# The state-space mixer of a decoder layer in chunks of 64 tokens, two chunks in the partition halves

## The chip, the core and the metric

The kernel runs on one core of one Trainium2 chip. The time is the device time of one launch in microseconds, from the first to the last instruction and what the launch lays around them; smaller is better. The core has five engines that run side by side[...]: TensorE (PE, with the weight load shown apart as PEld), VectorE (DVE), ScalarE (ACT), GpSimd (POOL) and SyncE (SP), which here only issues transfers. The on-chip memory has 128 partitions; TensorE writes to PSUM, eight banks of 2 KB a partition. All data are float32.

## What is computed

One decoder layer on x of 4 x 1024 tokens and 256 features, in three stages, each followed by the addition of its input and a layer norm without weights:

1. a mixer with 16 heads of 16 channels and a state of 64, which is the part that changes;
2. cross attention over 77 context tokens, with a mask;
3. a feed-forward of 256 to 1024 to 256 with relu.

The mixer in the reference, cut to what matters:

```
logA = einsum(W_logA, x) + b_logA                 # one number per token and head
XBC  = silu(einsum(W_XBC, x) + b_XBC)             # X: 16, B: 64, C: 64 per token and head
cum  = cumsum(logA over the tokens)
A    = where(causal, exp(cum_i - cum_j), 0)       # per head, 1024 x 1024
G    = einsum('bihn,bjhn->bhij', C, B)
Y    = einsum('bhij,bjhc->bihc', A * G, X)
out  = (gate * Y) @ W_out.T + b_out               # gate is linear in x
```

No 1024 x 1024 matrix has to be built. The tokens are cut into chunks: inside a chunk the product A * G is formed as it stands, and what earlier chunks contribute is carried by a state of 64 x 16 per head, which decays by the exponential of the chunk's last cum and takes in the chunk's own B and X.

## The kernel before

**Tiling.** The 4096 tokens are 16 units of T = 256 tokens, four to a batch. In the mixer a unit has NC = 2 chunks of P = 128 tokens. `stage_a(u)` is the mixer, `stage_b(u)` the attention, `stage_c(u)` the feed-forward of unit u.

**Order.** Nothing is ordered by the loops. Every piece of work is a small function that `part(u, name)` puts on a list with a place: u plus the number that `WHEN[name]` holds, or `EDGE[u][name]` for units 0, 1 and 15. The list is sorted by place and the functions are called in that order, so that each engine gets its instructions in it. Place is counted in units: a name at -0.7 is issued 0.7 of a unit before the unit's number. Several units are in flight at once, and the matmuls of the feed-forward of one stand between the mixer's steps of another. Waits between engines are put in from the tiles' reads and writes. PSUM is one pool of eight banks (`bank`).

**The steps of the mixer**, with their lines in the old kernel:

- `pl` (589), `cum` (600): logA for all heads, tokens along the free axis, and its running sum on VectorE, each chunk from 0. Partition 64 c + 32 k + h holds head h of group k in chunk c.
- `cd`, `dl` (606 to 623): cum goes out to DRAM and comes back broadcast to all partitions: `dl` is 128 (token j) x 8 heads x 128 (token i) for a chunk c and a group k of 8 heads. `ce`, `ec` (611 to 633): the same values by head and channel, for the decay of the state's part.
- `pcum`, `ncum` (636, 643): -cum with tokens on the partitions, as a bias.
- `ex`, `sel` (787, 796): exp(cum_i - cum_j) per head on ScalarE, in place, and zeros above the diagonal on GpSimd.
- `pb`, `th`, `bct` (661 to 690): B and C by a matmul, and silu on ScalarE and VectorE. A `bct` tile holds two heads, 64 rows each.
- `pg` (806), `st` (818): G for a chunk and a group of 8 heads, and the product with A on VectorE. B is loaded as weights, C moves. A matmul has 64 rows, one of two heads, so two run on the array's two row halves; 128 columns move.
- `ptb`, `bk` (825, 833): B turned, tokens on the partitions. `xw` (772): X times the decay to the end of the chunk.
- `pc`, `sn` (857, 870): the chunk's own part of the new state, and the new state as the old one decayed plus that part. `pts`, `new` (883, 893): the state turned and copied, in the form in which `pyo` needs it as weights.
- `pyo`, `py` (842, 904): the old state times C, and X times (A * G). Weights are 128 rows x 32 columns, so four run side by side on the array's column quarters; 128 columns move.
- `ya`, `yg`, `poa`, `r1` (916 to 945): the two parts added, the gate, the output projection, the residual.

The state is stepped once a chunk, twice a unit; `states[chunk % 2]` and `statesT[chunk % 2]` are the old one, the other two the new one. At a batch's first chunk there is no old state (`first`), at its last no new one is made (`last`).

**Shapes of the array.** A matmul is given a tile of the 128 x 128 array by the rows of its weights (128, 64 or 32) and by their columns (128, 64 or 32). Consecutive matmuls on different tiles of one shape can run side by side.

## Time and profile before

| | |
|---|---|
| median of 3 runs | 707.78 us (707.65 to 707.82) |
| the profiled execution | 708.88 us |
| its span, first to last instruction | 707.2 us |
| mean granted TensorE clock | 0.99 |
| instructions | 19482 |
| HBM read, written | 55.50 MB, 6.29 MB |

The costliest groups of TensorE besides the feed-forward (busy us, number of passes): pg 70.0, 1024; pb 43.5, 1024; pe 35.5, 512; ptb 35.2, 224; py on dl 34.8, 1024; pa 34.2, 512; py on the state 18.1, 448; pc 17.9, 448; pts 11.0, 56. The feed-forward's pf and ph take 121.5 and 120.1, with 512 passes each.

How to read it: the page is one execution. Busy times of TensorE contain the time in which a matmul is only on its way through the array, so that neighbours overlap and the sum of the lengths is more than the time; the start times tell how fast matmuls follow each other. A share of busy time is a mean over the span. Idle time of an engine other than the one that sets the end costs nothing.

### The profile page before, as it was taken

How to read it: one execution, taken by the hardware profiler on the slowest of the kernel's cores; microseconds unless marked ns; L12 is line 12 of the kernel's file. 1: busy time of each engine (PE TensorE's matmuls, PEld its weight loads, DVE VectorE, ACT ScalarE, POOL GpSimd, SP SyncE). 2: the span in 40 equal slices, each digit the busy share in tenths (PEclk: the TensorE clock that was granted, in tenths of full speed). 3: DMA queues.
4: the chain of work that ended last, by engine and by line, in shares of the span. 5: the costliest groups of instructions: out<-in, count | busy, mean ns of one | idle time of the engine just before them, and what ended most of it. 6: DMA issues, size and time to landing. Idle time of an engine off the chain costs nothing.

```text
span 707.2 us, 19482 instructions
## 1 busy us (share of the span) xinstructions
PE 676.7 (96%) x7744; PEld 536.2 (76%) x7744; DVE 542.9 (77%) x1336; ACT 414.9 (59%) x1091; POOL 276.9 (39%) x448
## 2 busy tenths in 40 slices
PE   0888999999999999999999999999999999999996
PEld 0556777877878787887878788787878888787785
DVE  1469989687878787887977787887878788786662
ACT  0566877557575674738577565846666474763210
POOL 0533353433344353334444344334425333443241
PEclk9989999999999999999999999999999999999999
DMA  4464573314131232413321231342322122100001
GB/s 110 111 192 145 161 231 130 79 62 127 61 112 62 69 97 69 144 60 110 102 76 68 93 111 61 83 135 78 107 96 84 65 79 76 39 9 9 16 8 38
DMA packets 40438, 63.05 MB, mean 89 GB/s; under 512 B 6095, under 2 KB 29340, under 8 KB 40348
## 3 DMA queue, kind: packets, MB, share of 16 engines
q1 hardware_dynamic: 38880, 61.40, 28.2%
q8 instruction: 61, 1.00, 0.6%
q10 hardware_dynamic: 1468, 0.41, 0.3%
q14 instruction: 29, 0.24, 0.1%
HBM read 55.50 MB, written 6.29 MB: 87 GB/s over the span
## 4 chain that ended last, share of the span: by engine, by line
PE 91%; DVE 5%; DMA 2%; issue 1%; POOL 1%; SPq 0%; POOLq 0%; ACT 0%; DVEq 0%
PE pf L1157 16%; PE ph L1130 16%; PE pg L813 9%; PE pb L668 5%; PE pe L1039 5%; PE pa L1064 4%; PE po_b L1100 4%; PE pq L967 4%; PE po_a L937 4%; PE py L910 4%; PE ptb L831 4%; PE pm L992 3%; PE px L730 2%; PE py L849 2%; PE pgt L697 2%; PE pc L864 2%
## 5 line engine op out<-in xcount | busy, mean ns | idle before, releaser
L791 ACT ACTIVATE dl<-dl,ncum 128x128 f32<-128x128 f32 x512 | 156.0, 393 | 8.2 <-DVE de L763 8.2
L1157 PE MATMUL pf<-w,hT 128*128 128x256 f32 x512 | 121.5, 382 | 0.0
L1130 PE MATMUL ph<-T_c,w 128*128 128x256 f32 x512 | 120.1, 381 | 0.0
L799 POOL TENSOR_SCALAR_AFFINE_SELECT dl<-dl 128x1024 f32<-128x1024 f32 x64 | 70.1, 1095 | 112.7 <-ACT dl L791 103.4
L1130 PEld LDWEIGHTS ph<-T_c,w 128*128 128x128 f32 x512 | 95.1, 190 | 14.6 <-issue 2.5
L1157 PEld LDWEIGHTS pf<-w,hT 128*128 128x128 f32 x512 | 93.7, 190 | 13.1 <-issue 1.8
L1050 ACT ACTIVATE es<-pe,mb 77x512 f32<-77x512 f32 x128 | 77.0, 680 | 45.3 <-PE pe L1039 44.1
L688 DVE SCALAR_TENSOR_TENSOR bct<-th,pb 128x512 f32<-128x512 f32 x128 | 81.7, 679 | 9.0 <-ACT th L680 8.9
L838 ACT COPY bk<-ptb 128x512 f32<-128x512 f32 x56 | 32.8, 586 | 92.8 <-PE ptb L831 92.7
L823 DVE TENSOR_TENSOR dl<-pg,dl 128x512 f32<-128x512 f32 x128 | 80.9, 682 | 6.7 <-PE pg L813 4.9
L680 ACT ACTIVATE th<-pb 128x512 f32<-128x512 f32 x128 | 69.3, 591 | 23.0 <-PE pb L668 19.1
L813 PE MATMUL pg<-bct 64*128 64x128 f32 x1024 | 70.0, 284 | 0.5 <-DVE bct L688 0.4
L813 PEld LDWEIGHTS pg<-bct 64*128 64x128 f32 x1024 | 62.5, 191 | 9.3 <-DVE mv_b L542 2.5
L1003 DVE TENSOR_REDUCE maxes<-pm 128x4 f32<-128x308 f32 x128 | 52.2, 470 | 14.4 <-PE pm L992 14.3
L1146 ACT ACTIVATE hT<-ph,b 128x256 f32<-128x256 f32 x64 | 26.7, 471 | 48.8 <-PE ph L1130 47.7
L547 POOL TENSOR_SCALAR rs_a<-mv_a 128x1 f32<-128x1 f32 x32 | 7.3, 228 | 113.4 <-DVE mv_a L542 113.4
L931 POOL TENSOR_TENSOR yg<-ya,gT 128x256 f32<-128x256 f32 x28 | 21.7, 776 | 67.4 <-DVE ya L924 51.9
L668 PE MATMUL pb<-xt,w_bc 17*64 17x256 f32 x1024 | 43.5, 408 | 1.6 <-DVE dl L823 1.4
L1082 POOL TENSOR_TENSOR on<-at,rec 128x256 f32<-128x256 f32 x32 | 19.8, 618 | 46.3 <-DVE rec L1077 44.5
L668 PEld LDWEIGHTS pb<-xt,w_bc 17*64 17x64 f32 x1024 | 22.6, 137 | 18.6 <-issue 9.9
L831 PE MATMUL ptb<-ident,bct 128*128 128x128 f32 x224 | 35.2, 282 | 1.3 <-DVE dl L823 1.2
L1039 PE MATMUL pe<-qm,kT 32*77 32x256 f32 x512 | 35.5, 389 | 0.0
(124 smaller groups left out, 1214.5 us busy)
## 6 DMA issues: line engine op xcount, KB each, us to landing
dl<-cd SPq DMA_DIRECT2D x64, 512.0 KB
xt<-in_xT_dram SPq DMA_DIRECT2D x64, 64.0 KB
xu<-in_xT_dram SPq DMA_DIRECT2D x16, 256.0 KB
ec<-ce SPq DMA_DIRECT2D x16, 256.0 KB
xk<-in_x_dram SPq DMA_DIRECT2D x16, 256.0 KB
out_dram<-r SPq DMA_DIRECT2D x32, 128.0 KB
w<-in_w_dram SPq DMA_DIRECT2D x2, 1024.0 KB
cd<-cum SPq DMA_DIRECT2D x16, 64.0 KB
```

The source lines that it names most:

```text
L668: nc.tensor.matmul(pbs[r][64 * half : 64 * half + 64, bc, :], lhsT=w_bc[rs, 2 * gk + half, bc, :], rhs=xt[rs, 2 * gk + half, :], start=Tru ...
L680: nc.scalar.activation(th, s[f"pb{gk}"][r], AF.Tanh)
L688: nc.vector.scalar_tensor_tensor(t, s[f"th{gk}{r}"], 1.0, s[f"pb{gk}"][r], ALU.add, ALU.mult)
L791: nc.scalar.activation(dl[:, h, :], dl[:, h, :], AF.Exp, bias=s["ncum"][:, 2 * c + k, h : h + 1],)
L799: nc.gpsimd.affine_select(out=dl, in_=dl, compare_op=ALU.is_ge, fill=0.0, base=0, pattern=[[0, 8], [1, P]], channel_multiplier=-1,)
L813: nc.tensor.matmul(pgs[half][:, r, :], lhsT=t[lo : lo + 64, 0, cs], rhs=t[lo : lo + 64, 1, cs], start=True, stop=True,)
L823: nc.vector.tensor_tensor(d, v[f"pg{k}"][half], d, ALU.mult)
L831: nc.tensor.transpose(v[f"ptb{k}"][:, r, :], s["bct"][4 * k + r][:, 0, cs], ident)
L1039: nc.tensor.matmul(pes[r][:, par, :], lhsT=kT[rs, gp, par, bs], rhs=s["qm"][rs, par, gp, :], start=True, stop=True,)
L1050: nc.scalar.activation(e, s[f"pe{gp}"][r], AF.Exp, bias=mb[:, b : b + 1], scale=CH**-0.5)
L1130: nc.tensor.matmul(ph[:, j, :], lhsT=w1[:, k, f * P : (f + 1) * P], rhs=s["xT"][:, k, :], start=(k == 0), stop=(k == 1),)
L1157: nc.tensor.matmul(pf, lhsT=s["hT"][:, f, c * P : (c + 1) * P], rhs=w2[:, f, :], start=(f == 0), stop=(f == FF // P - 1),)
```

## The change

The mixer's chunk becomes L = 64 tokens. Two chunks are handled together, one in each half of the partitions: c still counts 128 tokens, and a new index q counts its halves.

- `pl` and `cum`: one partition group of 32 for each of the four chunks of a unit, all 16 heads in it, 64 tokens along the free axis. `pl` sums two matmuls per chunk.
- `dl`: one tile per c for all 16 heads, 128 x 2 x 8 x 64: the partitions 64 q to 64 q + 63 get the chunk 2 c + q. Two transfers of 256 KB each. `ec`: two transfers instead of one, same size in sum.
- `pcum`: instead of one transposition, two matmuls with columns of the identity, one into each half of the partitions.
- `ex`: as many instructions, 64 columns each. `sel`: two instructions per (c, k), one for each half of the partitions.
- `pg`: a matmul has 64 rows (one of two heads) and 64 columns of weights (the tokens of one half), and 64 columns move: array quarters. Twice as many. `st`: two instructions per c instead of four, of the same size.
- `pc`: weights of 64 rows x 32 columns: array eighths, 128 columns move, twice as many, into two banks. `sn`, `pts`, `new`: the state is stepped for q = 0 and then q = 1: four steps a unit. `ptb`, `bk` and `xw` are no longer left out in a batch's last chunk, where the step for q = 0 is still made.
- `py`: weights of 64 rows x 32 columns, 64 columns move: eighths, twice as many, into two banks. `pyo`: weights of 128 rows x 32 columns as before, 64 columns move, twice as many. The half q = 1 uses the state that this same c made for q = 0.
- `ya`: two instructions per q, four per c, each of half the size.
- `states`, `statesT`: two halves each. `dl` has 4 buffers of the same size instead of 5 with one tile per c instead of two.
- `WHEN` and `EDGE`: all numbers are new, those of the attention and the feed-forward too. Among them: the context's loads and the first of its values stand ahead of the mixer's first inputs.

The core of the diff:

```diff
+L = 64
@@ chunk_a
-        old, new = states[chunk % 2], states[(chunk + 1) % 2]
-        so, sn = statesT[chunk % 2], statesT[(chunk + 1) % 2]
+        old, new = states[(chunk + 1) % 2], states[chunk % 2]
+        so, sn = statesT[(chunk + 1) % 2], statesT[chunk % 2]
+        before = [(None if first else old[:, 1], None if first else so[:, 1]), (new[:, 0], sn[:, 0])]
+        kept = range(1 if last else 2)
...
+        @part(u, f"pg{c}")
+        def _():
+            pgs = v["pg"] = [bank([P, 2, 4, L], f"pg_{n}_{a}") for a in range(2)]
+            for k in range(2):
+                for r in range(4):
+                    t = s["bct"][4 * k + r]
+                    for a in range(2):
+                        for q in range(2):
+                            ts = slice(c * P + q * L, c * P + q * L + L)
+                            nc.tensor.matmul(
+                                pgs[a][L * q : L * q + L, k, r, :],
+                                lhsT=t[64 * a : 64 * a + 64, 0, ts],
+                                rhs=t[64 * a : 64 * a + 64, 1, ts], start=True, stop=True,
+                            )
...
+        @part(u, f"pc{c}")
+        def _():
+            v["pc"] = [bank([P, 2, P], f"pc_{n}_{q}") for q in kept]
+            for k in range(2):
+                for q in kept:
+                    js = slice(L * q, L * q + L)
+                    for r in range(4):
+                        nc.tensor.matmul(
+                            v["pc"][q][32 * r : 32 * r + 32, k, :],
+                            lhsT=v["xw"][js, 4 * k + r].rearrange("p a c -> p (a c)"),
+                            rhs=v[f"bk{k}"][js, r, :], start=True, stop=True,
+                        )
+        @part(u, f"sn{c}")
+        def _():
+            for q in kept:
+                if before[q][1] is None:
+                    nc.vector.tensor_copy(sn[:, q], v["pc"][q])
+                    continue
+                for k in range(2):
+                    nc.vector.scalar_tensor_tensor(
+                        sn[:, q, k, :], before[q][1][:, k, :], s["ec"][:, k, c, q, L - 1 : L],
+                        v["pc"][q][:, k, :], ALU.mult, ALU.add,
+                    )
...
+        @part(u, f"pyo{c}")
+        def _():
+            py = pys()
+            for q in range(2):
+                if before[q][0] is None:
+                    continue
+                for k in range(2):
+                    for r in range(4):
+                        nc.tensor.matmul(
+                            py[q][32 * r : 32 * r + 32, 0, k, :],
+                            lhsT=before[q][0][:, 4 * k + r].rearrange("n a c -> n (a c)"),
+                            rhs=s["bct"][4 * k + r][:, 1, c * P + q * L : c * P + q * L + L],
+                            start=True, stop=True,
+                        )
+        @part(u, f"py{c}")
+        def _():
+            py = pys()
+            for k in range(2):
+                for half in range(2):
+                    for q in range(2):
+                        js = slice(L * q, L * q + L)
+                        for r in range(4):
+                            nc.tensor.matmul(
+                                py[q][32 * r : 32 * r + 32, 1, k, :],
+                                lhsT=xz[js, half, 4 * k + r, :],
+                                rhs=s[f"dl{c}"][js, k, 2 * r + half, :],
+                                start=(half == 0), stop=(half == 1),
+                            )
```

## The prediction

> **What bounds the kernel now.** I read the page from the top: the engine shares, then the slices, then one stretch in the middle, then the rows of one engine in order of time.

> ```profile
> span 707.2 us, 19482 instructions
> PE 676.7 (96%) x7744; PEld 536.2 (76%) x7744; DVE 542.9 (77%) x1336; ACT 414.9 (59%) x1091; POOL 276.9 (39%) x448
> PE   0888999999999999999999999999999999999996
> PE 91%; DVE 5%; DMA 2%; issue 1%; POOL 1%; SPq 0%; POOLq 0%; ACT 0%; DVEq 0%
> ```

> TensorE is busy from the second slice to the last, and 91% of the chain that ended last is TensorE. The busy times of the stretch 267.02 to 308.13, which is one of the 16 units (the same place in the order comes round again after 41.1 us), in the order PE, PEld, DVE, ACT, POOL, clock, DMA share, GB/s:

> ```profile
> 267.02:308.13 41.11, 41.11 (x505) 33.12 (x497) 32.55 (x83) 26.23 (x69) 16.27 (x25) 1.00 0.28 91
> ```

> TensorE has no idle time in it, at full clock; VectorE, the next, has 8.5 us to spare. So only what TensorE does, or would newly wait for, moves the time. Its rows (start, length):

> ```profile
> 341.75 1.89 PE L1157 MATMUL pf<-w,hT 128*128 128x256 f32 x8
> 343.57 0.81 PE L992 MATMUL pm<-km,q 32*128 32x154 f32 x16
> 344.31 1.99 PE L1157 MATMUL pf<-w,hT 128*128 128x256 f32 x8
> 346.24 0.81 PE L992 MATMUL pm<-km,q 32*128 32x154 f32 x16
> 346.97 1.08 PE L910 MATMUL py<-dl,xz 128*32 128x128 f32 x32
> 347.87 0.62 PE L864 MATMUL pc<-bk,xw 128*32 128x128 f32 x16
> 348.42 2.06 PE L813 MATMUL pg<-bct 64*128 64x128 f32 x32
> 350.40 0.66 PE L1016 MATMUL pmt<-ident,maxes 128*128 128x128 f32 x4
> ```

> Lengths contain the pipeline; what counts is start to start. A float32 matmul is two passes (32 records for 16 matmuls of pg). Passes on different tiles of the array start 7 ns apart and run side by side; then the next round follows. From the starts of single records: a full-array pass over 256 columns takes 216 ns, a round of 154 columns 130, of 128 columns 109, so 0.84 ns a column and 2 more. px and pg take 112[...]. Check: py, 8 rounds of four at 109, is 0.87 us; the next row starts 0.90 later.

> A change of tile shape costs extra. pf, 8 passes x 216 = 1.73, but pm starts 1.82 later; pm, 4 rounds x 130 = 0.52, but pf starts 0.74 later: 0.31 for two changes. pg, 16 x 112 = 1.79, then 1.98: 0.19. Pairs of neighbours give 0.12 to 0.22; I take **0.17 us**. py to pc, one shape, costs nothing.

> The whole: all rounds make 603 us, and 290 changes of shape (counted in the program's order) 49; the other 55 are the first 16 us, a ragged start up to 60 us, and the tail.

> **The change, part by part, on TensorE.** A round of 64 columns should take 2 + 64 x 0.84 = 56 ns, 58 where it also loads 64 columns.

> - pg: 16 rounds of two tiles a chunk become 16 of four, 64 columns long. 512 x (112 - 58) = **-27.6**.
> - py on dl: 8 rounds of four become 8 of eight. 256 x (109 - 56) = **-13.6**. Eight starts at 6.8 ns fill 54 of these 56 ns.
> - py on the state: 112 rounds of 109 become 240 of 56 (half 1 of a batch's first chunk now has one): **+1.2**.
> - pc: 112 rounds of four become 112 of eight and, in four last chunks, 16 of four, still 128 columns: **+1.8**.
> - pts: four transposes a chunk for two, 120 for 56: 64 x 109 = **+7.0**. ptb no longer skips a batch's last chunk: 32 x 109 = **+3.5**.
> - pl and pcum: twice the matmuls, half the columns or fewer: 0.

> Sum of rounds **-27.7**. Then the shapes. py on dl (64 rows x 32 columns) and on the state (128 x 32) no longer share one, and pc and pcum get their own: 373 changes for 290. 83 x 0.17 = **+14.1** (10 to 18 by the two ends). No profile row names this cost; it takes half of the gain.

> **Waits.** TensorE's separate semaphore waits go from 193 to 319. At 16 us, where four stand close together, they are 126 to 165 ns apart. If all 126 new ones were bare: +16. But in the middle of the run about 18 pairs of load and matmul are ahead of such a wait, which covers 0.25 us even at the new pace; I take **+3** (0 to 16).

> New in kind is the chain inside a chunk: pc, sn, pts, new, then the state product of half 1 of the same chunk. By rows: four sn steps at 0.30 (14.4 us for 48), pts 0.44 and 0.27 to drain, two copies at about 0.35: 2.6 us. The state had half a unit before; now, in the order built, pq, po_b, ptb and pm (about 4 us) stand between pc and pts, and po_b, pc of the other chunk and py (about 2) between pts and the product. The 4 us cover sn if VectorE comes to it within 2.8; the 2 us cover drain and copies (1.0) if ScalarE is free within 1. I take 0; uncovered by 1 us in 32 chunks, +32. The old trace has one such wait:

> ```profile
> PE pts L889 <- DVE stateT L878: 0.6, 1, 0.6
> ```

> **Other engines**, all beside TensorE. VectorE: st halves (64 of 682 ns fewer: wall -40), sn +19 (64 more steps at 0.30), ya +13 (four instructions of half size for two), the scan -3: 532, still 8 us free a unit. ScalarE: 512 exponentials of 64 columns for 128, about 40 ns less each, -20; more bk and a larger new, +8. GpSimd: 128 selects on half the partitions for 64, about as long in sum, and 4 more xw. dl is fetched in 64 transfers of half the bytes, ec in two per unit instead of one; DMA is at 28%. None of it decides unless TensorE gets a wait.

> **The start.** The order is new: on SP eight loads for the keys and values now stand ahead of xt and xu, and a later transfer waits for the one eight before it (k_b waited 5.5 us for v_w's load, issued at 8.4, to 17.4). So pl comes later than 16.0; but keys, values, and the projections of later units now stand before the first pg and fill what was ragged. I take **+2** (-5 to +8).

> Sum: -27.7 + 14.1 + 3 + 2 = **-8.6**: 698.6 for a span of 707.2. That run took 708.9, the median is 707.8; from the median, **699**.

> [...] The row first: passes on different tiles start 7 ns apart, in py four at a time. [...] What the row leaves open is a long run: no 64 passes in the old trace stand closer than 27 ns on average, while py now asks for 7. One place bounds the supply: after a wait that ended at 116.735 us TensorE's queue put out 12 pairs in 168 ns, so 14 ns a pair or less.

> **Rivals.**
> - *Supply of instructions* (17%). pg, pc and the state product have 14 ns a pair, py only 7. At 14 ns py gains nothing: +14, **713**; over 11.2 ns the kernel is slower than before. For it: 3344 more pairs in bursts never seen; against: the 12 pairs.
> - *The chain of states is late* (16%). 0.3 us in each of 32 chunks eats the gain; 0.5 us gives **715**. For it: two state steps in a row where there was one; against: the slack above.
> - *Quarters run two at a time* (8%), so that the change doesn't do what it says: pg then takes 32 rounds of 58, +29.7, **728**. Against it: pb already runs eight tiles side by side.
> - *More is hidden* (12%): cheap changes of shape (0.12) and a denser start: **688**.
> - My sum (47%), its own range 690 to 707.

> Within 0.2% (1.4 us, about what a measurement tells from no change) lies 0.04 from the edge of my sum's range. Faster: 0.44 of mine, all of the fourth, and 0.03 of a chain that is late by little, 0.59; slower 0.37. The range reaches to the first three: 685 to 728.

> **What would show it.** Right: pg's block of 64 records is followed 0.95 to 1.15 us later by its neighbour, py's on dl 0.45 to 0.65 later; a unit takes 40.2 us with TensorE still full. Supply: py's starts 10 ns or more apart. Chain: waits of pts on stateT or py on state in every unit. The start: the first slices show PE later than 16 us. The forecast is wrong if the middle unit exceeds 41.1 us, whatever the cause.

## The result, and the profile after

The kernel became slower by a third of a per cent: 709.87 us (708.38 to 713.34, 15 runs) for 707.82 (706.34 to 708.32, 15 runs) of the kernel before on the same chip, ratio 1.0035 with a 95% interval of 1.0021 to 1.0049. The forecast was 699. The runs after are also spread wider, 5.0 us for 2.0. The profiled execution took 708.51 us.

The page of the changed kernel, the lines that answer to those of before:

```profile
span 706.8 us, 26495 instructions
PE 665.4 (94%) x11088; PEld 524.1 (74%) x11088; DVE 515.3 (73%) x1402; ACT 403.4 (57%) x1107; POOL 296.0 (42%) x525
PE   1768979999999999999999999999999999999996
PE 90%; DMA 4%; issue 2%; DVE 1%; POOL 1%; SPq 0%; POOLq 0%; ACT 0%; ACTq 0%
```

The second, third and sixth slices lie lower than before (a slice is 17.7 us). The chain now has 4% of DMA for 2% before, and 2% of "issue" for 1%: time for which the profile names no wait. One unit in the middle, with the columns as before:

```profile
296.04:336.04 40.00, 40.00 (x691) 31.78 (x683) 30.75 (x85) 24.98 (x70) 17.79 (x32) 1.00 0.24 71
```

This unit takes 40.0 us, where the one shown before took 41.1, with TensorE full. It looks as if the middle gave what was forecast (40.2), but the units are not alike: at a batch's end the old kernel leaves some work out, and its units there take 39.5 and 40.7 us. A fair comparison is a whole batch, from the first pq of a unit to the first pq four units later, before and after:

```profile
296.94:459.37 162.43, 162.43 (x1931) 130.79 (x1930) 131.11 (x326) 103.32 (x274) 66.54 (x106) 1.00 0.28 87
296.04:456.75 160.71, 160.71 (x2774) 127.82 (x2767) 124.47 (x341) 100.54 (x276) 71.25 (x125) 1.00 0.22 64
```

That is 1.7 us a batch, or 0.43 a unit, half of the 0.85 that the sum of rounds and shapes promised. TensorE's rows in the unit:

```profile
305.92 0.31 PE L643 MATMUL pcum<-ident,cum 128*64 128x32 f32 x4
306.16 1.16 PE L834 MATMUL pg<-bct 64*64 64x64 f32 x64
307.25 1.22 PE L674 MATMUL pb<-xt,w_bc 17*64 17x256 f32 x32
...
310.40 0.60 PE L1030 MATMUL pmt<-ident,maxes 128*128 128x128 f32 x4
310.93 0.86 PE L923 MATMUL py<-dl,xz 64*32 64x64 f32 x64
311.72 0.65 PE L908 MATMUL py<-bct,state 128*32 128x64 f32 x32
312.31 1.99 PE L1144 MATMUL ph<-T_c,w 128*128 128x256 f32 x8
```

pg to its neighbour is 1.09 us, inside the forecast's 0.95 to 1.15: the quarters do run four at a time. py on dl takes 0.79, not 0.45 to 0.65. The starts of single records in that block say why: 32 passes stand in the first 0.27 us, mostly 7 ns apart as assumed, the other 32 take 0.52 with the change of shape at the end. From the 33rd on the starts come 16 to 17 ns apart, or 11 and 6 in turn.

TensorE's waits over the whole run (us in total, times, longest):

```profile
PE pl L594 <- DMA xu<-in_xT_dram: 20.2, 3, 13.2
PE pv L501 <- DMA kv_w<-in_v_w_dram: 4.8, 1, 4.8
PE py L923 <- issue: 4.1, 1, 4.1
PE pb L674 <- DVE vz L506: 1.8, 1, 1.8
PE pb L674 <- issue: 1.5, 1, 1.5
PE pg L834 <- issue: 1.4, 2, 0.8
```

There is no wait for a state in it. New are 7.0 us labelled "issue", in four stops between 58 and 117 us; the list of the old trace has none. The longest one, and the rows behind it:

```profile
87.72 0.66 PE L923 MATMUL py<-dl,xz 64*32 64x64 f32 x41
92.46 0.42 PE L923 MATMUL py<-dl,xz 64*32 64x64 f32 x23 [4.08 <-issue]
92.81 0.91 PE L908 MATMUL py<-bct,state 128*32 128x64 f32 x32
93.65 2.00 PE L1053 MATMUL pe<-qm,kT 32*77 32x256 f32 x16
```

py stops after 41 of its 64 passes, though the rest needs nothing that the first part did not have. (pe then takes 1.94 us to its neighbour, for 1.03 elsewhere.)

**Where the expected gain went.** For each stretch I take the elapsed time, less the rounds and 0.17 us a change of shape as in the prediction; what is left is lost time.

| us | before | after |
|---|---|---|
| rounds, whole run | 603.8 | 575.2 |
| 0.17 x changes of shape | 49.3 | 63.4 |
| lost, 0 to 140 us | 45.0 | 53.5 |
| lost, 140 to 680 us | 3.5 | 9.1 |

Rounds -28.6 (forecast -27.7) and shapes +14.1 stand as forecast. The losses took it all back: +8.5 in the first 140 us, of which 7.0 are the stops labelled "issue", and +5.6 in the middle, where 26 chunks lie and py takes 0.2 us longer than it should in each. Eight chunks make the 1.7 us that a batch is short.

### The profile page after: what moved, and what is told of

The parts are those of the page before. It is cut to its first block, busy times and chain, and to the rows that moved or that the text cites. A ratio compares the mean times of both kernels' runs of the same rounds, so it can differ in the third digit from the quotient of the medians.

```text
span 706.8 us, 26495 instructions
## 1 busy us (share of the span) xinstructions
PE 665.4 (94%) x11088; PEld 524.1 (74%) x11088; DVE 515.3 (73%) x1402; ACT 403.4 (57%) x1107; POOL 296.0 (42%) x525
## 4 chain that ended last, share of the span: by engine, by line
PE 90%; DMA 4%; issue 2%; DVE 1%; POOL 1%; SPq 0%; POOLq 0%; ACT 0%; ACTq 0%
PE ph L1144 16%; PE pf L1171 16%; PE pg L834 5%; PE po_a L951 5%; PE pe L1053 5%; PE pb L674 5%; PE pq L981 4%; PE pa L1078 4%; PE ptb L816 4%; PE po_b L1114 4%; PE py L923 3%; PE pm L1006 3%; DMA xu<-in_xT_dram 3%; PE pc L858 3%; PE py L908 2%; PE pts L881 2%
## 5 line engine op out<-in xcount | busy, mean ns | idle before, releaser
L798 ACT ACTIVATE dl<-dl,ncum 128x64 f32<-128x64 f32 x512 | 127.6, 337 | 0.4
L807 POOL TENSOR_SCALAR_AFFINE_SELECT dl<-dl 64x512 f32<-64x512 f32 x128 | 83.9, 655 | 83.7 <-ACT dl L798 79.4
L821 ACT COPY bk<-ptb 128x512 f32<-128x512 f32 x64 | 37.2, 585 | 67.7 <-PE ptb L816 55.2
L1155 DVE TENSOR_SCALAR hT<-ph,b 128x256 f32<-128x256 f32 x64 | 27.9, 478 | 28.0 <-PE ph L1144 28.0
L674 PE MATMUL pb<-xt,w_bc 17*64 17x256 f32 x1024 | 40.7, 396 | 4.9 <-DVE vz L506 1.8
L845 DVE TENSOR_TENSOR dl<-pg,dl 128x512 f32<-128x512 f32 x64 | 40.9, 680 | 6.1 <-PE pg L834 5.1
L871 DVE SCALAR_TENSOR_TENSOR stateT<-stateT,ec,pc 128x128 f32<-128x128 f32 x112 | 31.8, 341 | 11.2 <-PE pc L858 9.0
L816 PE MATMUL ptb<-ident,bct 128*128 128x128 f32 x256 | 39.8, 283 | 0.0
L834 PE MATMUL pg<-bct 64*64 64x64 f32 x2048 | 38.0, 221 | 1.5 <-issue 1.4
L834 PEld LDWEIGHTS pg<-bct 64*64 64x64 f32 x2048 | 33.3, 134 | 7.7 <-issue 6.6
L951 PE MATMUL po_a<-w_out,yg 128*128 128x256 f32 x128 | 37.2, 415 | 0.0
```

Of the source, the lines that this page charges most:

```text
L674: nc.tensor.matmul(pbs[r][64 * half : 64 * half + 64, bc, :], lhsT=w_bc[rs, 2 * gk + half, bc, :], rhs=xt[rs, 2 * gk + half, :], start=Tru ...
L798: nc.scalar.activation(dl[:, k, h, :], dl[:, k, h, :], AF.Exp, bias=s["ncum"][:, c, 8 * k + h : 8 * k + h + 1],)
L807: nc.gpsimd.affine_select(out=d, in_=d, compare_op=ALU.is_ge, fill=0.0, base=0, pattern=[[0, 8], [1, L]], channel_multiplier=-1,)
L816: nc.tensor.transpose(v[f"ptb{k}"][:, r, :], s["bct"][4 * k + r][:, 0, cs], ident)
L834: nc.tensor.matmul(pgs[a][L * q : L * q + L, k, r, :], lhsT=t[64 * a : 64 * a + 64, 0, ts], rhs=t[64 * a : 64 * a + 64, 1, ts], start=True ...
L951: nc.tensor.matmul(v["po"], lhsT=v["yg"][:, k, :], rhs=w_out[:, k, :], start=(k == 0), stop=(k == 1),)
```

## The experiments

The theory at this point: TensorE runs short of instructions, in two ways. In py it uses up those that stand ready, and the next ones come slower; and now and then it waits for a block of its program to be fetched. Counting both rows of a pass (weight load and matmul), TensorE has 15488 instructions before and 22176 after; the instruction queue whose packets go with these counts shows 61 and 88 of 16 KB, so 254 and 252 instructions each. The four stops end 1.3 to 1.6 us after such a packet is through (packets at 57.2, 82.5, 89.6 and 114.0 us). The rival: the new order of the start costs what is missing.

**1. The two weight loads spread.** w1 and w2 are 1 MB each and stand beside the stop at 88 us.

```diff
-        nc.sync.dma_start(out=w1, ...)      # s_1, place 0.69
-        nc.sync.dma_start(out=w2, ...)      # s_2, place 0.86
+        # four times, at 0.7, 1.0, 1.3, 1.6: a quarter of w1, a quarter of w2
```

> The changed kernel, with the loads of w1 and w2 (1 MB each, issued together at 83 to 88 us) cut into eight pieces of 256 KB that go out in pairs, 10 us apart. Theory (the stop of 4.1 us inside py at 88.2 us is TensorE waiting for its own instructions, whose 16 KB transfer at 89.6 stands beside the two large loads): the stop goes, no stop of TensorE labelled 'issue' over 1 us is left after 80 us, and the time falls by 4 to 5.5 us, to about 705 from 709.9. Rival (the stop comes from the program, or from something in py itself): the stop stays within 1 us of its length and the time changes by less than 1 us. Rival (TensorE is late at the start anyway, and the stop only fills a gap that would come later): the stop goes, and the time falls by less than 1.5 us.

710.27 us (705.22 to 716.2, 22 runs), ratio 1.003 (1.0016 to 1.0045): no gain. The stops sum to 7.2 us, now in six pieces. Four stand ahead of the same blocks as before (pb at 61, pg at 86, py at 91, pg at 115 us), two are new (1.2 us in py at 121, 1.1 in pb at 429). The one in py fell from 4.1 to 1.9 us, and its packet, counted in the same way, started 3.2 us after that first instruction instead of 4.9. So the loads go with the length of that stop, but they are not what makes the stops, and the expectation failed. The rival from the program is right on the places and wrong on the length.

**2. The old order of the start**, and **3. both edits and xu(2) early.**

```diff
-    "s_c": -17.7488, "s_x": -14.3181, ... "keys": -6.9902, "values0": -5.1040,
+    "s_c": -14.5, "s_x": -17.7, ... "keys": -3.54, "values0": -3.51,
+    2: {"load_u": -4.36},      # EDGE, run 3 only
```

> The changed kernel with the order of before at the start: xt, xu and the mixer's weights first, then the eight context loads; keys, values and the eight loads of b_g behind the first pl. Theory (pl(0) waits for xu(0), which stands behind eight loads on SP): pl(0) starts at 16 us instead of 19.9, everything behind it comes 3 to 4 us earlier, and the time falls by 2.5 to 5 us, to about 706. Rival (the start is not what costs: the keys and values are then late themselves, or the stretch from 20 to 60 us is bound by the chain behind pl): pl(0) starts earlier but the last TensorE instruction moves by less than 1 us.

> Both edits of the two runs before it, and in addition the load of xu(2) moved up behind that of xu(1), so that pl(2) no longer waits 5.6 us for it at 43 to 49 us. Theory (start and instruction fetch are the two terms that the prediction had too small, +6.5 us together, and the steady part gives its gain): about 699 to 702, thus faster than both kernels, ratio to before 0.986 to 0.992. Rival (the gain of a steady unit, 1.1 us, is not worth 16 units, because something fills up elsewhere): 704 to 709.

Run 2: 713.96 (711.52 to 717.39), ratio 1.0096 (1.0073 to 1.012), slower. pl starts at 15.7 instead of 19.9, and TensorE then stands 7.5 us before the keys, whose weights GpSimd has not laid out yet. Run 3: 708.99 (702.72 to 712.78), ratio 1.0009 (0.999 to 1.0029), the rival's value. Both still have 6.8 us of stops. So the start's order was not the missing term.

**4. py issued twice.** If the slow half of py belongs to the supply, more passes show its price.

```diff
+            for again in range(2):
                 for k in range(2):
```

> The changed kernel with the matmuls of weighted X (py on dl) issued twice, the second time over the first, with the same result: 64 passes more in each of 32 chunks, no change of shape more. By my sum (56 ns a round of eight, 8 rounds): +14.3 us. By the supply theory (TensorE's queue holds about 30 passes ahead; behind these they come 16.6 ns apart, whatever their tiles): 64 passes at 16.6 ns, +1.06 us a chunk, +34 us, and at least 10 ns a pass, +20 us; the second 64 starts all stand 16 to 17 ns apart or 11 and 6 in turn. If the slow part belonged to py's tiles and not to the queue, the second 64 would repeat the first 64: 30 starts 7 ns apart, then slower, +0.62 us a chunk, +20 us.

769.1 us (one run), +59 over the changed kernel, more than any of the three. In the order of time, a chunk with a stop (114 passes, and then the other 14) and one without:

```profile
434.14 1.36 PE L924 MATMUL py<-dl,xz 64*32 64x64 f32 x114
436.24 0.34 PE L924 MATMUL py<-dl,xz 64*32 64x64 f32 x14 [0.73 <-issue]
...
476.82 1.48 PE L924 MATMUL py<-dl,xz 64*32 64x64 f32 x128
478.23 0.65 PE L908 MATMUL py<-bct,state 128*32 128x64 f32 x32
```

128 passes take 1.41 us and 64 took 0.79, so 64 more cost 0.62, or 9.7 ns a pass where the sum had 7: +20 us in 32 chunks. The size alone does not tell the supply from the tiles, since 0.62 is just what the expectation gave for the tiles. The starts do: in the block at 476.82 us the first 32 passes come mostly 7 ns apart, and the second 64 do not begin so again; they go on at 16 to 17, 11 and 6, with some pairs 0 to 1 apart. Right behind a stop passes come mostly 7 ns apart again, in the middle of a block. Most of the rest is stops, now in the middle of the run as well:

```profile
PE py L924 <- issue: 13.1, 10, 2.4
PE py L908 <- issue: 8.7, 5, 2.4
PE pb L674 <- issue: 4.5, 2, 3.9
PE pm L1007 <- issue: 3.9, 3, 1.5
PE ph L1145 <- issue: 1.5, 1, 1.5
```

31.7 us for 7.0, with no change to any transfer of data. More instructions alone bring the stops. Some 15 of the 59 us have no row of their own. Most of them go with the clock: in stretches with a granted clock of 0.50 TensorE is busy for 42.2 us here and for 15.5 in the changed kernel. At half speed 26.7 us more are worth at most 13 us, by an estimate from these figures.

**5. and 6. A copy of 1 MB in ten middle units**, in both kernels.

```diff
+    for u in range(4, 14):     # 1 MB of w1 to a spare place in DRAM
+        jobs.append((u - 0.75, len(jobs), f"copy_{u}", copy))   # before: u - 0.40
```

> The changed kernel with one more transfer in each of ten middle units (4 to 13): 1 MB copied from DRAM to a spare place in DRAM that nothing reads, issued by ScalarE's queue just ahead of the dense stretch of pg, pc and py. TensorE's program is the same. Theory (TensorE executes 256 instructions per 16 KB fetched, and a transfer of instructions that stands beside a full load of the DMA engines comes later than the dense stretch can wait): stops labelled 'issue' now turn up in the middle units, where the profile of the changed kernel has none, 1 to 4 us each, +8 to +30 us in all. Rival (fetching has nothing to do with it, the stops at the start come from the start's own order): no stops labelled 'issue' between 160 and 560 us; less than +5 us, from later data alone.

> The same ten copies of 1 MB in the kernel before, which has 30% fewer TensorE instructions and no stretch with so many of them together. Theory (fetch): no stops labelled 'issue', or under a third of those of the changed kernel, +0 to +5 us. Rival (the copies hold up data, not instructions): the same loss as in the changed kernel within 3 us.

The kernel before does not feel the copies: 707.11, ratio 0.9993 (0.9985 to 1.0001), no stop. The changed kernel goes to 714.74 (709.15 to 718.32, 5 runs), ratio 1.009 (1.0056 to 1.0123). Its profile has four stops in the middle, where it had none (0.93, 0.22, 1.26 and 0.49 us), 9.5 us in all, and 14.0 us lost between 140 and 680 us for 9.1. So the copies do hurt the kernel with many instructions and not the other. The rival without a fetch falls, but the effect is below the 8 us that I expected at the least, and the stops are 2.9 of the 4.9 us in the middle.

**7. A third order of the start**, with the keys behind the mixer's first steps.

> The changed kernel with the start ordered anew: xt, xu and the mixer's weights first, then b_g, then the context loads, the keys and the values behind px(0) and pgt(0) of unit 0, and xu(2) loaded right behind xu(1). Against the earlier run with both edits this takes away the 7.3 us that TensorE stood before the keys' weights and the 3.0 us before gT. Theory (the start's data waits and the stops for instructions are separate losses): the data waits of 20 to 50 us fall by 5 us or more, the stops labelled 'issue' stay at 5 to 9 us, and the time is 702 to 707. Rival (what is won ahead of 50 us is waited for behind it, because the dense stretches then follow each other faster and run out of instructions): the stops grow by as much as the data waits shrink, 707 to 711.

710.17 (704.9 to 715.37, 22 runs), ratio 1.0038 (1.0018 to 1.0057). The time is the rival's. Its reason is not shown: the stops grew only to 8.4 us, and the data waits did not shrink, since pb now stood 4.2 us for ScalarE's work on the keys.

**8. Half of py left out** (the odd heads' part inside a chunk).

> The changed kernel without the odd heads' part of weighted X inside a chunk (half of py on dl is left out: 32 passes instead of 64 in each of 32 chunks, 2048 TensorE instructions of 22,000 fewer). By my sum (4 rounds of 56 ns a chunk): -7.2 us, 702.7. By the supply theory (the passes left out are those that come at 9.75 ns and more, and with fewer instructions fewer stops for the fetch): -10 us from the passes and 2 to 6 us from the stops, 694 to 698.

691.3 us (690.67 to 692.39), ratio 0.9771 (0.9758 to 0.9785): -18.6 for 1024 passes, below the supply theory's own range, and two and a half times what the rounds are worth. The 32 passes take 0.38 us to the neighbour, the change of shape included, where 64 took 0.79, and behind pc 0.54 for 0.86: the second 32 passes are the dear ones. At 0.36 a chunk that is -11.5; stops go from 7.0 to 3.4. Of the 3.5 us that remain some 2 go with the clock, by the same estimate as in run 4 (busy at half clock for 11.2 us instead of 15.5).

**9. The same work in half the passes.** Nothing is left out here. The two heads of a row group of y are stacked in the two partition halves, and one matmul on 128 rows takes the place of two on 64 that were added up. For the second chunk the halves are swapped, so that pg keeps its four tiles.

```diff
# pg
-  pgs[a][L * q : L * q + L, k, r, :]
+  pgs[q][L * (a ^ q) : L * (a ^ q) + L, k, r, :]
# py
-  for half in range(2): for q in range(2): for r in range(4):
-      matmul(py[q][...], lhsT=xz[js, half, 4 * k + r, :], rhs=dl[js, k, 2 * r + half, :],
-             start=(half == 0), stop=(half == 1))
+  for q in range(2): for r in range(4):
+      matmul(py[q][...], lhsT=xz[:, q, 4 * k + r, :], rhs=dl[:, k, 4 * q + r, :])
# xz: X of head parity `half`, chunk q, to partition half b
+  b = half ^ q
+  nc.gpsimd.tensor_copy(xz[L * b : L * b + L, q, :, CH * half : CH * half + CH], thx[L * q : ...])
# dl by partition half b: heads of parity b ^ q; -cum to match; de from its own small transpose
```

> The changed kernel with weighted X on quarters of 128 rows by 32 columns instead of eighths: the two heads that share a row group of y are stacked in the two partition halves (for the second chunk the halves are swapped, so that pg still runs on four tiles), their X goes into one zero-padded weight of 128 rows, and one matmul takes the place of two that were added up. py on dl has the same 8 rounds of 56 ns a chunk, but 32 passes instead of 64; nothing is left out. It costs four copies more a chunk on GpSimd, two transfers more a chunk, 8 small passes more a unit, and saves two VectorE steps a chunk and 16 changes of tile shape. By my sum (only rounds and shapes count): -2.7 for the shapes and +1 for the small passes, 708. By the supply theory (a pass beyond those that the queue holds costs 9.75 ns and not 7, and 4096 instructions more make TensorE stop for its fetches): 8 to 13 us less, 696 to 701, with stops labelled 'issue' under 4 us.

> The same, with the order of the start as in the run before that moved the mixer's inputs ahead and xu(2) up. If the instructions were what took back the better start there, it shows now: 2 to 4 us below the run without it, 693 to 698. If not, the same time within 1.5 us.

704.61 (702.62 to 706.82), ratio 0.9958 (0.9941 to 0.9975): faster than both kernels, but short of 696 to 701. (py gives up 2048 instructions, and the small transposes add 256; the 4096 in the expectation was miscounted.) The stops are 1.8 us, and the middle loses 0.8 us in 120 as before the change. One stretch does not, and its wait is new:

```profile
PE pc L879 <- ACT bk L844: 2.6, 1, 2.6
```

ScalarE stood 7.2 us at 562 us because a tile of thx now lives until GpSimd has made xw of it, and there were two. The other start (706.2, 702.68 to 708.71) brings nothing here either.

**10. A third buffer for thx**, alone and with xu(2) early.

```diff
-  v["thx"] = tile_([P, H * CH], "thx", f"thx_{n}")
+  v["thx"] = tile_([P, H * CH], "thx", f"thx_{n}", bufs=3)
```

> The stacked version with a third buffer for thx. In its profile ScalarE stood 7.2 us at 562 us, because thx now holds X until GpSimd has made xw from it and the next tanh had no buffer, and TensorE stood 2.6 us before pc for that (bk late); the stretch of 500 to 620 us lost 5.6 us for 0.8 in the others. Theory (that stand is all that kept the stacked version above the 696 to 701 expected): the loss in 500 to 620 us falls to about 1 us and the time to 700 to 702. Rival (the stand fills a gap that comes later anyway, in the tail): less than 1.5 us better, 703 to 705.

> The same with the load of xu(2) issued right behind that of xu(1), so that pl(2) doesn't wait 5 to 7 us for it at 43 to 50 us. With 12% fewer instructions than in the changed kernel TensorE has fetches in hand, so if the stops were what took back the better starts there, 2 to 4 us less than the run beside it, 697 to 700. Rival (the start up to 80 us is bound by more than one thing: the chain of scan, transfers and exponentials behind each pl): within 1.5 us of it.

**698.08 us** (697.27 to 698.98), ratio 0.9857 (0.9842 to 0.9871): 1.4% faster than the kernel before and 11.8 us faster than the changed one. That is below the 700 to 702 expected, and the rival of the tail falls. Stops 1.1 us, lost time of 500 to 620 us 1.5. A batch, counted as above, and its py:

```profile
289.47:448.61 159.14, 159.14 (x2551) 126.24 (x2543) 125.42 (x328) 100.48 (x276) 80.81 (x157) 1.00 0.23 65
```

```profile
295.45 0.65 PE L942 MATMUL py<-dl,xz 128*32 128x64 f32 x32
295.92 0.63 PE L929 MATMUL py<-bct,state 128*32 128x64 f32 x32
296.48 0.81 PE L1024 MATMUL pm<-km,q 32*128 32x154 f32 x16
```

py and pyo now share a shape and take 1.03 us together, for 1.38 in the changed kernel (310.93 to 312.31). A batch is 3.3 us shorter than in the old kernel. xu(2) early gives 698.58 (696.1 to 699.55), no difference: pl(2) no longer waits, and pc and pv wait 3.8 and 2.8 us instead (TensorE has 8% fewer instructions than in the changed kernel, not the 12 of the expectation). The start is bound by more than one thing.

## Why the prediction was wrong

- **pg, quarters (-27.6): right.** 1.09 us from block to neighbour; the rival that they run two at a time falls. The rounds of four start 58 ns apart, as the sum had it, for 112 in the old pg. Why a round of px or the old pg takes 3 ns more than one of py is not shown: ptb, whose passes load 128 columns of weights too, takes 109.
- **Changes of shape (+14.1): right by the sum, not tested alone.** With 0.17 us each, the middle of the stacked kernel closes to 0.8 us in 120, like the kernel before. The price itself was not varied in a run of its own.
- **The start (+2): right by what is left.** Of +8.5 us up to 140 us, 7.0 are stops for instructions; 1.5 remain, and of these some 0.9 go with the clock, by the estimate of run 4 (busy at half clock for 15.5 us, 13.6 in the old kernel). Three other orders of it brought nothing.
- **Separate waits (+3) and the chain of states (0).** No wait on a state is seen. The stacked kernel loses no more in the middle than the one before, so the added waits cost about nothing there.
- **py on dl (-13.6): wrong, and with it the price of the supply, which stood at nothing.** The prediction weighed a supply of 14 ns a pass as a rival and argued it down by one place: after a wait that ended at 116.735 us TensorE's queue put out 12 pairs in 168 ns. That was the step that failed. The place allows 14 ns a pair, twice the 7 that py needs, and 12 pairs are fewer than the number that come quickly anyway. It could say nothing of 64 in a row. (Whether those 12 had been lying ready is not shown.) The new py shows both paces in one block: about 30 passes mostly 7 ns apart, then 16 to 17 or 11 and 6 in turn. That a queue holds the first 30 was my theory in the expectations; the traces show the two paces, not what sets the number. Sustained, a pass costs 9.7 ns for py (64 more passes in run 4), less than the rival's 14: it cost the middle +5.6 us, about half of what py was to give there. The prediction's own sign, a unit of 40.2 us, could not catch it, since 41.1 is not the mean of the old units but 40.6.
- **The fetch of the program was in no case of the prediction: a term put at nothing.** It took 7.0 us in the profiled run, which is among the fastest of the 15. The spread of these runs goes with the granted clock: the three slowest (712.7 to 713.3) have 0.976, the twelve others 0.981 to 0.985. Whether the stops make the clock fall is not shown.

-28.6 + 14.1 + 5.6 + 7.0 + 1.5 is -0.4, and the span went from 707.2 to 706.8; the median lies 1.4 us above the profiled run. The rival "supply of instructions" had the right cause, by two mechanisms where it named one. That its 713 came near 709.9 is partly luck: its price of a pass was too high, and the fetch, which it did not have, made up for that.

What stays open: what sets the moment at which a packet of instructions starts. In the changed kernel it ranges from 3.9 us ahead of the first instruction of the block before its own to 4.9 us behind it. The stops fall with fewer instructions and rise with more (31.7 us in run 4, 3.4 in run 8, 1.8 in run 9, for 7.0), and the copies of run 5 took them from 7.0 to 9.5 us, but taking the largest loads away from one did not lower their sum (1).

## What to carry to other kernels

When a change cuts a TensorE operation into smaller tiles, count its instructions as well as its rounds: here the passes beyond the first 30 or so in a row cost 9.7 ns each, by run 4, where their rounds need 7, and the waits for the program took 7.0 us. Look how long the shortest 256 instructions take (at 5.0 us nothing stopped here, at 2.7 to 3.7 some did). And look for a stacking that fills the rows instead (two 64-row matmuls that are added up are one of 128 rows): here it kept the gain of 64-token chunks with half the passes and turned 0.3% slower into 1.4% faster. Take a rate of supply only from a stretch as long as the one that you plan. And compare whole periods of the work, here a batch, not one unit that looks typical.

## What the runs showed that I had not expected

Behind the longest stop the clock is lower. In the four microseconds of the stop at 88 us and the four behind it (columns as in the lines of the unit and the batch, the clock third from the end):

```profile
88.00:92.00 4.00, 0.38 (x34) 0.21 (x11) 2.51 (x4) 3.58 (x12) 0.10 (x1) 1.00 1.06 257
92.00:96.00 4.00, 3.54 (x72) 2.23 (x73) 2.26 (x6) 0.33 (x1) 0.73 (x1) 0.63 1.07 242
```

The granted clock is 0.63 right behind it, and pe there takes 1.94 us instead of 1.03. So another 0.9 us is lost right behind the stop; whether the stop lowers the clock is not shown. The old kernel, without a stop, has 0.50 from 95.6 to 99.0 us. And a steady middle without any named wait still hid 5.6 us: TensorE shows as busy 539.99 of 540 us while py's passes came late, since their lengths overlap. Only the starts of the records showed it.
